# Two layers of attention on one core: layer 1's maxima and sums sent through DRAM, its weights a step later

## The chip, the cores and the metric

The kernel runs on one core of one Trainium2 chip. The metric is the time of one execution on the device in microseconds (us). The profile is of one further execution; the engines are named as in it: PE (matrix products), PEld (its weight loads), DVE (vector), ACT (scalar), POOL (GpSimd) and SP (here only a queue for DMAs).

## The reference, cut to what matters

Two attention layers over an image of 2 x 256 x 64 x 64 in float32, that is 2 batches of N = 4096 positions with 256 channels. Layer 0 (layer norm, four heads of 16 channels, a gate, a sigmoid) is not touched. Layer 1 is this:

```
qkv = einsum('oc,bchw->bohw', w_qkv, x) + b_qkv        # 4 heads, each 3 x 64 channels
q, k, v = split(qkv.reshape(b, 4, 192, 4096), 3, axis=2)
attn = softmax(einsum('bhdn,bhdm->bhnm', q, k) / sqrt(64), axis=-1)
out = einsum('bhnm,bhdm->bhnd', attn, v).reshape(b, c, h, w)
return einsum('oc,bchw->bohw', w_out, out) + b_out + x
```

## The kernel before, in words

Layer 1 works through 32 units `(b, g, j)`: a batch, a pair of heads, and a block of NB = 512 queries. A unit has NM = 32 chunks of 128 keys. A chunk's scores for both heads are one tile of 128 keys x (2 heads x 512 queries). Two chunks are done in one step `t`, so a unit takes 16 steps, and the body of layer 1 has 512.

The softmax subtracts a maximum, and it does so by halves: the 16 chunks of a half (`GS`) share one maximum for each query and head. A half's exponentials can't begin before its last scores are in, so scores run ahead: the shift and the exponential of a chunk come `LAG` = 10 steps after its scores, and the product with the values one step later. In between the scores lie in a ring of 2 LAG + 4 = 24 buffers in SBUF.

For each chunk:

- PE multiplies keys by queries into a "pair" buffer in PSUM (`score`, L861). There are two of these, of two banks each.
- DVE takes the running maximum over the chunks, element by element (`keep`, L878), and ACT copies the scores into the ring (L879). The copy waits for the maximum of the same chunk, and PE's scores two chunks on wait for the copy.
- LAG steps later DVE adds the negated maximum (`shift`, L944), ACT takes the exponential in place (`weigh`, L956), POOL adds it to an accumulator, from which the sum over the keys is made (L966 for the first two chunks of a half in one instruction, L968 for the others), and PE multiplies it with the values (`gather`, L978).

At the end of each half the maxima go through this chain:

1. `turn_max` (L886): PE transposes the 512 columns of one head into the single "misc" bank of PSUM, and `fold` (L898) lets DVE take the negated maximum over the 128 keys. This is done for one head at the step's "early" place and for the other at its "late" place.
2. `split` (L909 to L912): POOL takes each maximum apart into three bf16 pieces.
3. `turn` (L925, L930), a step later: PE turns the pieces into rows, ACT copies these to SBUF.
4. `spread_shift` (L939), a further step later: PE multiplies the rows by ones, which adds the pieces up and puts the result on all 128 partitions, in the single "shift" buffer of PSUM.

At the end of a unit, in steps 12 to 14 of the next one, come the sums. `total` (L1008): PE sums the accumulators over the partitions. `keep_total` (L1016): ACT copies that. `turn_total` (L1023): PE turns it. `factors` (L1035 to L1039): DVE joins the sums of the two halves and takes the reciprocal, POOL makes the other half's factor. `turn_sums` (L1023) and `rows` (L1049, L1056, L1060): PE turns the products with the values, DVE scales them, POOL adds the bias and the two halves together, and SP sends the result to DRAM (L1076). The last unit's rows go straight into the SBUF tile from which the last output is made (L1067).

Beside this, other steps hang in the loop: the queries of the next unit (`next_queries`, L672, at steps 14 and 15), and, in the first 24 units, keys and values for the unit eight further on (L672 and L705, at steps 4 to 7), which go to DRAM and are fetched back. During four units of the second batch the first batch's output is made as well (`project_out`, L1083, and `output`, L1091).

The order is written out by hand. `at(t, place, step)` hangs a step on a step number and a place (start, early, early end, late, late end), the main loop (L1219) runs through them, and `seq` keeps each engine's instructions in the program's order. Each engine, and SP, therefore takes its instructions one after the other: what waits holds up all that is behind it on the same engine. Tiles come from pools: a new tile in a pool waits until an older one's readers are done.

Of the kernel before, what the change touches and what calls it, by code (L numbers as in the profile page):

```python
# [9 lines left out]
BF16 = mybir.dt.bfloat16  # L10
# [17 lines left out]
def conv_attention_kernel(  # L28
# [149 lines left out]
    def layer1_constants():  # L178
# [25 lines left out]
        ident16 = const.tile([P, P], BF16, tag="ident16", name="ident16")  # L204
        nc.gpsimd.tensor_copy(ident16, ident)
        ones16 = const.tile([P, P], BF16, tag="ones16", name="ones16")
        nc.gpsimd.memset(ones16, 1.0)
        ones = const.tile([P, D1], F32, tag="ones", name="ones")
        nc.gpsimd.memset(ones, 1.0)


        negmax1 = []
        for i in range(2):
            t = const.tile([P, PB, P], BF16, tag=f"negmax1_{i}", name=f"negmax1_{i}")
            nc.gpsimd.memset(t, 0.0)
            negmax1.append(t)
        return w1, wo1, b1, b1v, bo1, ident16, ones16, ones, negmax1
# [27 lines left out]
    with own0:  # L245
# [412 lines left out]
        w1, wo1, b1, b1v, bo1, ident16, ones16, ones, negmax1 = layer1_constants()  # L658
# [109 lines left out]

    units = [(b, g, j) for b in range(B) for g in range(PR) for j in range(NJ)]
    GS = NM // 2  # L770
    NG = NM // GS
    LAG = GS // 2 + 2
# [5 lines left out]
    with (  # L778
# [9 lines left out]
        rmax, negs, mrows, shifts, raws, accs = {}, {}, {}, {}, {}, {}  # L788
        avs1, srows, losts, joined, halves = {}, {}, {}, {}, {}
        rts = [None, None]  # L790
# [10 lines left out]
        )  # L801
        last_att = []
# [78 lines left out]
        def turn_max(u, n, k):  # L881

            b, g, j = u
            ps = misc(f"rt_{b}_{g}_{j}_{n}_{k}")
            for i in range(PB):
                seq(nc.tensor.transpose(  # L886
                    ps[:, bass.ts(i, P)], rmax[u, n][:, k, bass.ts(i, P)], ident
                ))
            rts[k] = ps

        def fold(u, n, k):

            b, g, j = u
            if k == 0:
                negs[u, n] = small.tile(
                    [P, 2, PB], F32, tag="negs", bufs=2 * NG, name=f"negs_{b}_{g}_{j}_{n}"
                )
            seq(nc.vector.tensor_reduce(  # L898
                negs[u, n][:, k, :], rts[k].rearrange("p (i m) -> p i m", m=P), AX.X, ALU.max,
                negate=True,  # L900
            ))

        def split(u, n):

            b, g, j = u
            nm = negs[u, n]
            to = negmax1[n % 2].rearrange("p i (k e) -> p k i e", e=D1)
            rest = small.tile([P, 2, PB], F32, tag="rest1", name=f"rest1_{b}_{g}_{j}_{n}")
            seq(nc.gpsimd.tensor_copy(to[:, :, :, 0], nm))  # L909
            seq(nc.gpsimd.tensor_tensor(rest, nm, to[:, :, :, 0], ALU.subtract))  # L910
            seq(nc.gpsimd.tensor_copy(to[:, :, :, 1], rest))
            seq(nc.gpsimd.tensor_tensor(to[:, :, :, 2], rest, to[:, :, :, 1], ALU.subtract))  # L912
            if n == 1:

                lost = small.tile([P, 2, PB], F32, tag="lost", name=f"lost_{b}_{g}_{j}")
                seq(nc.gpsimd.tensor_tensor(lost, nm, negs.pop((u, 0)), ALU.subtract))
                negs.pop((u, 1))
                losts[u] = lost

        def turn(u, n):  # L920

            b, g, j = u
            ps = misc(f"nm1p_{b}_{g}_{j}_{n}")
            for i in range(PB):
                seq(nc.tensor.matmul(  # L925
                    ps[:, bass.ts(i, P)], negmax1[n % 2][:, i, :], ident16,
                    start=True, stop=True,
                ))
            mrows[u, n] = l1.tile([P, NB], BF16, tag="mrow", name=f"mrow_{b}_{g}_{j}_{n}")
            seq(nc.scalar.copy(mrows[u, n], ps))  # L930

        def spread_shift(u, n):

            b, g, j = u
            ps = psb.tile([P, 2, NB], F32, tag="shift", name=f"shift_{b}_{g}_{j}_{n}")
            row = mrows.pop((u, n))
            for k in range(2):
                r = slice(k * D1, (k + 1) * D1)
                seq(nc.tensor.matmul(ps[:, k, :], ones16[r, :], row[r, :], start=True, stop=True))  # L939
            shifts[u, n] = ps  # L940
# [72 lines left out]
        def keep_total(u):  # L1013
            b, g, j = u
            row = l1.tile([P, NB], F32, tag="srow", bufs=1, name=f"srow_{b}_{g}_{j}")
            seq(nc.scalar.copy(row, srows[u]))  # L1016
            srows[u] = row
            seq(nc.scalar.activation(losts[u], losts[u], AF.Exp, scale=D1**-0.5))

        def turned(a, name):  # L1020
            ps = misc(name)
            for i in range(PB):
                seq(nc.tensor.transpose(ps[:, bass.ts(i, P)], a[:, bass.ts(i, P)], ident))  # L1023
            return ps.rearrange("p (i k d) -> p i k d", k=2, d=D1)

        def turn_total(u):
            srows[u] = turned(srows[u], "sumt_{}_{}_{}".format(*u))

        def factors(u):

            b, g, j = u
            ps = srows.pop(u)
            lost = losts.pop(u).rearrange("p k i -> p i k")
            s = small.tile([P, PB, 2], F32, tag="sum1", name=f"sum1_{b}_{g}_{j}")
            seq(nc.vector.tensor_tensor(s, ps[:, :, 0, ::32], lost, ALU.mult))  # L1035
            seq(nc.vector.tensor_tensor(s, s, ps[:, :, 1, ::32], ALU.add))
            f = small.tile([P, NG, PB, 2], F32, tag="f1", name=f"f1_{b}_{g}_{j}")
            seq(nc.vector.reciprocal(f[:, 1], s))
# [6 lines left out]
        def rows(u, n):  # L1045
            b, g, j = u
            ps = avs1.pop((u, n))
            r = l1.tile([P, PB, 2, D1], F32, tag="rows", name=f"rows_{b}_{g}_{j}_{n}")
            seq(nc.vector.tensor_tensor(  # L1049
                r, ps, joined[u][:, n].unsqueeze(3).to_broadcast([P, PB, 2, D1]), ALU.mult  # L1050
            ))
            last = u == units[-1]
            if n == 1:
                halves[u] = r
                bias = b1v[:, 2 * g : 2 * g + 2, :].unsqueeze(1).to_broadcast([P, PB, 2, D1])
# [7 lines left out]
            if last:  # L1063
                for k in range(2):
                    c = ((2 * g + k) * N + j * NB) // D1 % P
                    for i in range(PB):
                        (nc.sync if k else nc.scalar).dma_start(  # L1067
                            out=last_att[0][c + 2 * i : c + 2 * i + 2, :].rearrange(
                                "q (s d) -> q s d", d=D1
                            ),  # L1070
                            in_=r[:, i, k, :],
                        )
                return
            to = att[b].rearrange("(h q) (s d) -> h (q s) d", h=H, d=D1)
            for k in range(2):
                nc.sync.dma_start(  # L1076
                    out=to[2 * g + k, bass.ts(j, NB), :].rearrange("(i q) d -> q i d", q=P),
                    in_=r[:, :, k, :],
                )

# [18 lines left out]
        def fetch_output(b, j):  # L1099
            fetch(("xo", b, j), x1[b][j], "xo", 2, l1)  # L1100
# [8 lines left out]
        for n, u in enumerate(units):  # L1109
            b, g, j = u  # L1110
            t0 = n * US
            if n > 0:
                at(t0 - 5, "start", lambda u=u, b=b, j=j: fetch(("q", u), x1[b][j]))
                at(t0 - 2, "late", lambda u=u: next_queries(u, 0))
                at(t0 - 1, "early", lambda u=u: next_queries(u, 1))
                at(t0 - 1, "early end", lambda u=u: keep_queries(u))
            if n < len(units) - NJ:
                to = (*units[n + NJ][:2], j)
                at(t0 + 1, "start", lambda to=to: fetch(("kv", *to), x1[to[0]][to[2]]))
# [185 lines left out]
```

## Time and profile before

| | us |
|---|---|
| median of 3 runs (lowest, highest) | 4742.67 (4740.17, 4742.81) |
| the profiled execution | 4741.58 |
| its span | 4739.8 |
| PE busy in the span | 4526.9 (96%) |
| DVE busy | 3917.0 (83%) |
| ACT busy | 3394.1 (72%) |
| POOL busy | 2540.6 (54%) |

The shares are means over both layers. Layer 1's loop begins near 2050 us and its last instructions end the run; POOL and DVE do most of their work there. The mean time of one instruction in layer 1: an accumulation on POOL 2.37 us, a shift 1.21, a maximum 1.22, a fold 0.69, a copy of scores on ACT 1.01, an exponential 1.06. In an answer of the trace each line of a timeline has its start, its length, engine, line, operation, what it writes and reads, and, in brackets, how long the engine stood idle before it and who released it. In a line of waits stand who waited for whom, the total, how often, and the longest.

### The profile page before, as it was taken

What the parts mean: (1) busy time and instruction counts of PE and PEld (TensorE: products, weight loads), DVE (VectorE), ACT (ScalarE), POOL (GpSimd) and SP (SyncE); (2) the same over time, 40 slices, a digit from 0 to 9 for tenths busy, and PEclk for the clock granted to TensorE, in tenths of its full rate; (3) what the DMA queues carried; (4) which work ended last, traced back from release to release, by engine and by line L of the source; (5) the groups of instructions that cost most, each with busy time, mean ns of one, the idle gap of its engine ahead of it and who ended that gap; (6) DMA issues with size and microseconds to landing.
All of it is one profiled execution on the core that took longest, in us unless ns stands there. A gap on an engine that the chain in (4) does not pass through costs nothing.

```text
span 4739.8 us, 70643 instructions
## 1 busy us (share of the span) xinstructions
PE 4526.9 (96%) x27506; PEld 1496.2 (32%) x27506; DVE 3917.0 (83%) x4584; ACT 3394.1 (72%) x4508; POOL 2540.6 (54%) x1491
## 2 busy tenths in 40 slices
PE   8999999999999999989999999999999999999998
PEld 3433333333333333333232232323233332222222
DVE  6777777777777777359999999999999899999996
ACT  3366666666666666668888888888887778888884
POOL 6300000000000000039999999999998889999994
PEclk9999999999999999999999999999999999999999
DMA  3100000000000000110000100001111111000002
GB/s 103 34 4 19 19 21 15 15 15 15 15 15 15 15 13 13 57 63 25 23 25 17 54 30 23 25 23 36 52 36 45 63 52 47 18 14 7 14 16 74
DMA packets 113381, 140.10 MB, mean 30 GB/s; under 512 B 51864, under 2 KB 52696, under 8 KB 112932
## 3 DMA queue, kind: packets, MB, share of 16 engines
q1 hardware_dynamic: 111260, 135.11, 9.2%
q8 instruction: 216, 3.54, 0.3%
q14 instruction: 121, 0.99, 0.1%
q10 hardware_dynamic: 1784, 0.46, 0.0%
HBM read 93.58 MB, written 41.70 MB: 29 GB/s over the span
## 4 chain that ended last, share of the span: by engine, by line
PE 58%; DVE 15%; POOL 15%; issue 6%; ACT 5%; DMA 1%; SPq 0%; ACTq 0%; DVEq 0%; POOLq 0%
PE s L448 24%; POOL acc L968 13%; PE av L463 12%; DVE rmax L878 10%; PE s L861 6%; PE av L978 5%; DVE raw L944 4%; ACT raw L879 4%; PE a L410 2%; PE p L270 1%; PE k1p L672 1%; POOL acc L966 1%; PE rt L886 1%; PE q1p L672 1%; PE o L549 1%
## 5 line engine op out<-in xcount | busy, mean ns | idle before, releaser
L968 POOL TENSOR_TENSOR acc<-acc,raw 128x1024 f32<-128x1024 f32 x884 | 2098.1, 2373 | 89.4 <-ACT raw L956 30.2
L414 DVE TENSOR_REDUCE mx<-a 128x1 f32<-128x512 f32 x2048 | 1315.3, 686 | 450.5 <-PE a L410 449.4
L451 ACT ACTIVATE p<-s 128x512 f32<-128x512 f32 x2048 | 1109.8, 597 | 701.3 <-PE a L410 367.3
L944 DVE TENSOR_TENSOR raw<-raw,shift 128x1024 f32<-128x1024 f32 x1024 | 1238.0, 1213 | 19.2 <-PE shift L939 12.7
L861 PE MATMUL s<-q,k 64*128 64x512 f32 x4096 | 1117.2, 636 | 142.9 <-ACT raw L879 134.6
L878 DVE TENSOR_TENSOR rmax<-s,rmax 128x1024 f32<-128x1024 f32 x960 | 1170.1, 1219 | 72.7 <-PE s L861 70.8
L879 ACT COPY raw<-s 128x1024 f32<-128x1024 f32 x1024 | 1037.7, 1013 | 259.4 <-DVE rmax L878 173.5
L448 PE MATMUL s<-q,kT 32*128 32x512 f32 x4096 | 1219.1, 640 | 0.0
L956 ACT ACTIVATE raw<-raw 128x1024 f32<-128x1024 f32 x1024 | 1086.9, 1062 | 178.4 <-DVE raw L944 147.3
L410 PE MATMUL a<-kT,q 32*128 32x512 f32 x4096 | 1129.7, 643 | 1.2 <-DVE mx L414 1.0
L978 PE MATMUL av<-raw,v 128*64 128x512 f32 x4096 | 999.3, 606 | 2.0
L463 PE MATMUL av<-p,v 128*32 128x256 f32 (+1 forms) x7904 | 650.2, 399 | 0.6 <-ACT avs L477 0.6
L861 PEld LDWEIGHTS s<-q,k 64*128 64x128 f32 x4096 | 317.1, 185 | 827.9 <-ACT raw L879 628.0
L513 POOL TENSOR_TENSOR f<-f,dyn 128x16 f32<-128x16 f32 x15 | 3.3, 223 | 1028.2 <-DVE f L512 1028.2
L448 PEld LDWEIGHTS s<-q,kT 32*128 32x128 f32 x4096 | 397.9, 183 | 426.3 <-issue 392.1
L978 PEld LDWEIGHTS av<-raw,v 128*64 128x64 f32 x4096 | 243.3, 136 | 587.6 <-issue 428.8
L463 PEld LDWEIGHTS av<-p,v 128*32 128x32 f32 x7904 | 157.6, 108 | 751.5 <-issue 737.3
L564 POOL TENSOR_SCALAR res<-res 128x1024 f32<-128x1024 f32 x16 | 16.8, 1049 | 660.5 <-ACT res L563 660.5
L410 PEld LDWEIGHTS a<-kT,q 32*128 32x128 f32 x4096 | 305.0, 184 | 31.4 <-DVE mx L414 18.2
L966 POOL TENSOR_TENSOR acc<-raw,raw 128x1024 f32<-128x1024 f32 x64 | 152.4, 2381 | 112.7 <-ACT raw L956 103.8
L898 DVE TENSOR_REDUCE negs<-rt 128x4 f32<-128x512 f32 x128 | 88.3, 690 | 50.1 <-PE rt L886 47.6
L318 DVE RECIPROCAL std<-std 128x128 f32<-128x128 f32 x64 | 56.1, 920 | 37.7 <-ACT std L313 37.7
(332 smaller groups left out, 1840.4 us busy)
## 6 DMA issues: line engine op xcount, KB each, us to landing
x<-in_x_dram SPq DMA_DIRECT2D x16, 512.0 KB
res<-in_x_dram SPq DMA_DIRECT2D x16, 512.0 KB
x<-res SPq DMA_DIRECT2D x16, 512.0 KB
att<-rows SPq DMA_DIRECT2D x62, 128.0 KB
kd<-k1s SPq DMA_DIRECT2D x24, 256.0 KB
vd<-v1s SPq DMA_DIRECT2D x24, 256.0 KB
k<-kd SPq DMA_DIRECT2D x24, 256.0 KB
v<-vd SPq DMA_DIRECT2D x24, 256.0 KB
```

The lines of the kernel that those rows point to most:

```text
L410: seq(nc.tensor.matmul(ps, qs0[u][r, bass.ts(i, P)], kTs[b][r, bass.ts(m, NB)], start=True, stop=True,))
L414: seq(nc.vector.tensor_reduce(mxs[u][:, i * H + h, m : m + 1], ps, AX.X, ALU.max))
L448: seq(nc.tensor.matmul(ps, kTs[b][r, bass.ts(m, P)], qs0[u][r, :], start=True, stop=True))
L451: seq(nc.scalar.activation(pt[:, k, :], ps, AF.Exp, scale=D0**-0.5))
L463: seq(nc.tensor.matmul(avs[u][32 * h : 32 * h + 32, cols], vs0[b][:, m, 32 * h : 32 * h + 32], pts[t, h // 2][:, h % 2, cols], start=(m == ...
L861: seq(nc.tensor.matmul(ps[:, k, :], ks[b, g, m // PB][r, bass.ts(m % PB, P)], qs1[u][r, :], start=True, stop=True,))
L878: seq(nc.vector.tensor_tensor(rmax[u, n], ps, before, ALU.max))
L879: seq(nc.scalar.copy(raw, ps))
L944: seq(nc.vector.tensor_tensor(raws[t], raws[t], shifts[u, t % NM // GS], ALU.add))
L956: seq(nc.scalar.activation(p, p, AF.Exp, scale=D1**-0.5))
L968: seq(nc.gpsimd.tensor_tensor(accs[u, n], accs[u, n], p, ALU.add))
L978: seq(nc.tensor.matmul(avs1[u, n][k * D1 : (k + 1) * D1, :], v[:, m % PB, k, :], raws[t][:, k, :], start=(m % GS == 0), stop=(m % GS == GS ...
```

## The change

The bf16 pieces and what belongs to them (`split`, `turn`, `spread_shift` and their constants) are taken out. `turn_max` transposes both heads at once into a "pair" buffer, taking every fourth query in a transpose, and one `fold` does both. SP sends the negated maxima to DRAM and reads them back onto all partitions (`row`); ACT copies that row into the "shift" buffer three steps after the fold (`place_shift`). LAG becomes 11, the ring gets 26 buffers. The sums go to DRAM and back as well, in place of `turn_total`, and two of the operations in `factors` move from DVE to POOL. Queries, keys, values and the outputs of the first batch are hung on other steps; there is one "xo" buffer in place of two. The last unit's rows go through DRAM.

```diff
-    LAG = GS // 2 + 2
+    LAG = GS // 2 + 3
...
+        def by_query(a, i):
+            return a.rearrange("p (q i) -> p i q", i=PB)[:, i, :]
...
+        def turn_max(u, n):
             b, g, j = u
-            ps = misc(f"rt_{b}_{g}_{j}_{n}_{k}")
-            for i in range(PB):
-                seq(nc.tensor.transpose(
-                    ps[:, bass.ts(i, P)], rmax[u, n][:, k, bass.ts(i, P)], ident
-                ))
-            rts[k] = ps
+            ps = psp.tile([P, 2, NB], F32, tag="pair", name=f"rt_{b}_{g}_{j}_{n}")
+            for k in range(2):
+                for i in range(PB):
+                    seq(nc.tensor.transpose(
+                        ps[:, k, bass.ts(i, P)], by_query(rmax[u, n][:, k, :], i), ident
+                    ))
+            rts[u] = ps
...
+        def fold(u, n):
+            nm = small.tile([P, 2, PB], F32, tag="negs", bufs=2 * NG, name=f"negs_{b}_{g}_{j}_{n}")
             seq(nc.vector.tensor_reduce(
-                negs[u, n][:, k, :], rts[k].rearrange("p (i m) -> p i m", m=P), AX.X, ALU.max,
-                negate=True,
+                nm, rts.pop(u).rearrange("p k (i m) -> p k i m", m=P), AX.X, ALU.max, negate=True,
             ))
+            to = neg1[u, n]
+            nc.sync.dma_start(out=to.rearrange("k (p i) -> p k i", i=PB), in_=nm)
+            row = l1.tile([P, 2, NB], F32, tag="row", bufs=1, name=f"row_{b}_{g}_{j}_{n}")
+            nc.sync.dma_start(
+                out=row.rearrange("p k n -> p (k n)"),
+                in_=to.rearrange("(o k) n -> o (k n)", o=1).partition_broadcast(P),
+            )
+            rows_in[u, n] = row
...
+        def place_shift(u, n):
             b, g, j = u
             ps = psb.tile([P, 2, NB], F32, tag="shift", name=f"shift_{b}_{g}_{j}_{n}")
-            row = mrows.pop((u, n))
-            for k in range(2):
-                r = slice(k * D1, (k + 1) * D1)
-                seq(nc.tensor.matmul(ps[:, k, :], ones16[r, :], row[r, :], start=True, stop=True))
+            seq(nc.scalar.copy(ps, rows_in.pop((u, n))))
             shifts[u, n] = ps
...
         def keep_total(u):
-            row = l1.tile([P, NB], F32, tag="srow", bufs=1, name=f"srow_{b}_{g}_{j}")
+            row = l1.tile([P, NB], F32, tag="kv", name=f"srow_{b}_{g}_{j}")
             seq(nc.scalar.copy(row, srows[u]))
-            srows[u] = row
+            for m in range(2 * NG):
+                nc.sync.dma_start(out=sum1[u][m : m + 1, :], in_=row[32 * m : 32 * m + 1, :])
+            s = small.tile([P, NG, 2, PB], F32, tag="sums1", name=f"sums1_{b}_{g}_{j}")
+            nc.sync.dma_start(
+                out=s.rearrange("p n k i -> p (n k) i"),
+                in_=sum1[u].rearrange("m (p i) -> p m i", i=PB),
+            )
+            srows[u] = s
...
         def factors(u):
-            seq(nc.vector.tensor_tensor(s, ps[:, :, 0, ::32], lost, ALU.mult))
-            seq(nc.vector.tensor_tensor(s, s, ps[:, :, 1, ::32], ALU.add))
-            f = small.tile([P, NG, PB, 2], F32, tag="f1", name=f"f1_{b}_{g}_{j}")
-            seq(nc.vector.reciprocal(f[:, 1], s))
+            seq(nc.gpsimd.tensor_tensor(s[:, 0], s[:, 0], lost, ALU.mult))
+            seq(nc.gpsimd.tensor_tensor(s[:, 1], s[:, 1], s[:, 0], ALU.add))
+            f = small.tile([P, NG, 2, PB], F32, tag="f1", name=f"f1_{b}_{g}_{j}")
+            seq(nc.vector.reciprocal(f[:, 1], s[:, 1]))
             seq(nc.gpsimd.tensor_tensor(f[:, 0], f[:, 1], lost, ALU.mult))
...
             for k in range(2):
-                nc.sync.dma_start(
-                    out=to[2 * g + k, bass.ts(j, NB), :].rearrange("(i q) d -> q i d", q=P),
-                    in_=r[:, :, k, :],
+                queue = (nc.sync, nc.scalar)[k if last else 0]
+                queue.dma_start(
+                    out=to[2 * g + k, bass.ts(j, NB), :].rearrange("(p i) d -> p i d", i=PB),
+                    in_=r[:, k, :, :],
                 )
+                if last:
+                    c = ((2 * g + k) * N + j * NB) // D1
+                    queue.dma_start(
+                        out=last_att[0][c % P : c % P + NB // D1, :],
+                        in_=att[b][c : c + NB // D1, :],
+                    )
...
-                at(t0 - 2, "late", lambda u=u: next_queries(u, 0))
-                at(t0 - 1, "early", lambda u=u: next_queries(u, 1))
-                at(t0 - 1, "early end", lambda u=u: keep_queries(u))
+                for c in range(CC):
+                    at(t0 - 6 + c, "early", lambda u=u, c=c: next_queries(u, c))
+                at(t0 - 5, "early end", lambda u=u: keep_queries(u))
...
-                    at(t0 + 4 + c, "early", lambda to=to, c=c: next_keys(*to, c))
-                at(t0 + 5, "early end", lambda to=to: store_keys(*to))
-                at(t0 + 6, "early", lambda to=to: next_values(*to, 0))
-                at(t0 + 7, "early", lambda to=to: next_values(*to, 2))
-                at(t0 + 7, "early end", lambda to=to: store_values(*to))
+                    at(t0 + 2 + c, "early", lambda to=to, c=c: next_keys(*to, c))
+                at(t0 + 3, "early end", lambda to=to: store_keys(*to))
+                at(t0 + 5, "early", lambda to=to: next_values(*to, 0))
+                at(t0 + 6, "early", lambda to=to: next_values(*to, 2))
+                at(t0 + 6, "early end", lambda to=to: store_values(*to))
...
-                at(t1, "early", lambda u=u, k=k: turn_max(u, k, 0))
-                at(t1, "early end", lambda u=u, k=k: fold(u, k, 0))
-                at(t1, "late", lambda u=u, k=k: turn_max(u, k, 1))
-                at(t1, "late end", lambda u=u, k=k: (fold(u, k, 1), split(u, k)))
-                at(t1 + 1, "late", lambda u=u, k=k: turn(u, k))
-                at(t1 + 2, "early", lambda u=u, k=k: spread_shift(u, k))
+                at(t1, "early", lambda u=u, k=k: turn_max(u, k))
+                at(t1, "early end", lambda u=u, k=k: fold(u, k))
+                at(t1 + 3, "start", lambda u=u, k=k: place_shift(u, k))
             t1 = t0 + US + GS // 2
             at(t1 + 4, "early", lambda u=u: total(u))
             at(t1 + 4, "early end", lambda u=u: keep_total(u))
-            at(t1 + 5, "early", lambda u=u: turn_total(u))
-            at(t1 + 5, "early end", lambda u=u: factors(u))
-            at(t1 + 5, "late", lambda u=u: turn_sums(u, 1))
-            at(t1 + 5, "late end", lambda u=u: rows(u, 1))
-            at(t1 + 6, "early", lambda u=u: turn_sums(u, 0))
-            at(t1 + 6, "early end", lambda u=u: rows(u, 0))
+            at(t1 + 6, "start", lambda u=u: factors(u))
+            for place, k in (("early", 1), ("late", 0)):
+                at(t1 + 6, place, lambda u=u, k=k: turn_sums(u, k))
+                at(t1 + 6, f"{place} end", lambda u=u, k=k: rows(u, k))
```

## The prediction

> **What bounds the kernel now.** First the busy share by stretch of the run, one line each from the body of layer 1 and from its last quarter (columns: stretch, length, then PE, weight loads, DVE, ACT, POOL, each with its instruction count, clock, DMA share, GB/s).
>
> ```profile
> 3000.00:3300.00 300.00, 283.74 (x1212) 90.57 (x1210) 280.81 (x267) 251.91 (x269) 280.05 (x156) 1.00 0.09 26
> 4200.00:4500.00 300.00, 275.75 (x1168) 82.17 (x1168) 288.06 (x274) 257.94 (x270) 286.42 (x158) 1.00 0.04 11
> ```
>
> PE, DVE and POOL are all at 93 to 96%, so shares don't say who is the bound. The waits between 2100 and 4600 us do (total, times, longest):
>
> ```profile
> DVE rmax L878 <- PE s L861: 66.3, 134, 0.9
> POOL acc L966 <- ACT raw L956: 92.0, 61, 2.5
> DVE negs L898 <- PE rt L886: 45.3, 61, 1.0
> ```
>
> POOL, once per half unit, has emptied its queue and waits 1.5 us for the first exponentials of the next half (L966). It is not ahead of anybody, but it isn't behind either: it follows DVE. So I read DVE's order of instructions in one unit; a unit of 16 steps runs from the fold at 3059.20 to the same one at 3140.64, 81.44 us.
>
> ```profile
> 3058.07 1.21 DVE L944 TENSOR_TENSOR raw<-raw,shift 128x1024 f32<-128x1024 f32 x1
> 3059.20 0.68 DVE L898 TENSOR_REDUCE negs<-rt 128x4 f32<-128x512 f32 x1
> 3059.80 1.22 DVE L878 TENSOR_TENSOR rmax<-s,rmax 128x1024 f32<-128x1024 f32 x1
> 3061.16 0.69 DVE L898 TENSOR_REDUCE negs<-rt 128x4 f32<-128x512 f32 x1
> ...
> 3067.42 1.22 DVE L878 TENSOR_TENSOR rmax<-s,rmax 128x1024 f32<-128x1024 f32 x1
> 3068.98 1.22 DVE L944 TENSOR_TENSOR raw<-raw,shift 128x1024 f32<-128x1024 f32 x1 [0.34 <-POOL acc L968]
> ...
> 3080.30 1.21 DVE L944 TENSOR_TENSOR raw<-raw,shift 128x1024 f32<-128x1024 f32 x1
> 3082.11 1.23 DVE L878 TENSOR_TENSOR rmax<-s,rmax 128x1024 f32<-128x1024 f32 x1 [0.60 <-PE s L861]
> ```
>
> Start to start, a shift or a maximum takes 1.13 us, a fold 0.60. 32 shifts and 31 maxima (71.4), four folds (2.4), two `rows` (1.2) and the three factor operations (0.5) make 75.6. The other 5.9 us are gaps in front of something late: 0.2 and 1.7 at the two pairs of folds (the second pair is the one at 3099.93 and 3102.38), 0.4 twice at the first shift of a half, 0.7 after the sums on PE, 2.2 behind the keys and values on PE, 0.3 elsewhere. DVE's order, with its gaps, is the clock of this stage; in the last quarter, without keys and values, DVE's sum (79.3) and POOL's (78.9 with 0.07 us between instructions) meet, and the unit takes 79.2.
>
> [...] the trace's exponential, from SBUF, takes 1.06. [...] in layer 0 a factor row is issued at 705.99 and its read-back at 708.24. [...] No PE read in the trace of before strides 16 bytes[...].
>
> **Part by part**, per unit, as changes of DVE's gaps.
>
> *Folds.* Two reduces of 1024 replace four of 512: 2.4 to 2 x 1.13 (priced as a tensor_tensor of that size), -0.14. The two small factor operations go to POOL: -0.4. Busy: -0.54.
>
> *The turned maxima move to a "pair" buffer.* Both pair buffers hold the scores of this step, so PE's transposes must wait for ACT's copy of the first. First half's end: the maximum starts at 3056.93 and ends 3058.16, ACT copies until 3059.2, eight transposes take 1.24 (two times the 0.65 of four, less overlap), the fold can start at 3060.6 where DVE is ready at 3059.2: wait 1.4, before 0.22, so +1.18. Second half's end: maximum 3095.47 to 3096.70, copy to 3097.7, exponential to 3098.9, copy of the new unit's first scores to 3099.9, transposes to 3101.2; DVE is ready at 3098.95: 2.35 against 1.69, +0.66. Queued behind the fold on DVE are the next maximum and shift, and behind the transposes on PE the gather; PE catches up behind the fold. If the 16-byte stride doubles the transposes, each wait grows by 1.2.
>
> *The shift is placed by ACT, a step later.* Its buffer (one) is free when DVE's last shift of the old half ends; ACT first does that chunk's exponential (1.06), then the copy into PSUM [...], while DVE has one maximum to do (1.06 more). Wait 1.1 instead of 0.4: +0.7, twice a unit. The row must be there[...]; DVE's order gives it 2.5 steps, some 12 us. [...]
>
> *The factors.* This is the largest. Before, DVE formed the sum itself. Now POOL multiplies and adds (two operations), and DVE's reciprocal waits for POOL, whose queue is in order: in front stand the accumulations of all chunks up to the one DVE has just shifted. What POOL has in hand there:
>
> ```profile
> 3073.99 2.38 POOL L966 TENSOR_TENSOR acc<-raw,raw 128x1024 f32<-128x1024 f32 x1 [2.54 <-ACT raw L956]
> 3076.45 12.17 POOL L968 TENSOR_TENSOR acc<-acc,raw 128x1024 f32<-128x1024 f32 x5
> 3088.58 0.20 POOL L1039 TENSOR_TENSOR f<-f,lost 128x8 f32<-128x8 f32 x1
> ```
>
> POOL is empty when the half's first accumulation (chunks 0 and 1, one instruction) comes; up to chunk 5 it needs 5 x 2.43, until 3086.15. The shift of chunk 5 starts at 3080.30 and DVE would take its next instruction at 3081.43: POOL is 4.7 us behind. Add two small operations at 0.28, subtract the gap of 0.68 behind the sums, which in the new order lies ahead of that shift: 4.6 us, each unit. Behind the reciprocal on DVE stand maximum, shift and `rows`; for the maximum waits ACT's copy, for that PE's scores. Bounds: 2 us if DVE arrives later through gaps I haven't seen, 5.5 with the sums' DMA late. That DMA (four issues, 1.39 us in layer 0[...]) has 9 us.
>
> *Moved PE work.* Queries go to steps 10 and 11 as an "early" step: a half before the gather costs 0.74 for keys, the second half lies in the placing's stall: 0.74 against 0.11, +0.63. The second half of the keys now lies in the other placing's stall: -0.27. Turned sums hide behind the reciprocal: -0.3. The removed PE work (turn, spread, turned totals, about 2.2 us) and POOL's four split operations with their gaps (2.3) are on engines that wait for DVE: nothing. [...] SP gets nine more issues a unit, under 4 us of 80, and each neg write is queued behind the att write, which waits for POOL's rows; those end at 3096 where the fold is at 3099.93, so nothing.
>
> *Ends.* LAG of 11 costs a step of drain, about 2.9 (gather 1.87 and sums 0.98); [...] the last rows now go out and back in four DMAs[...] where eight took from 4704.95 to 4718.5[...]. Sum 0.
>
> **Sum.** Reciprocal 31 x 4.6 = 143, less 8 in the four units of the output stage, where an output's wait ahead of it eats 1.9 each time; folds 31 x (1.18 + 0.66) = 57; placing 62 x 0.7 = 43; queries 20; busy -17; keys -6; turned -9. Together +223 on the profiled execution's 4741.6 (span 4739.8), which lies 1.1 under the median: 4965.
>
> **Rivals.** *Only the stalls at the folds and the placing count*: POOL would be relieved enough, or DVE late enough, that the reciprocal waits little. Without its 135: 4830. For it: POOL loses 1.8 us of work a unit. Against: it is already empty at each half's start, so it can't be further ahead. *The stride doubles the transposes*: 62 x 1.2 on top, 5040. [...] against it that weight loads (0.14) and transposes overlap. *Faster*: POOL is the bound, and DVE's new waits fall into time that it has spare anyway. Then POOL's relief counts, four split operations out, two in, 1.77 us x 32 = 57: 4685. It speaks for it that POOL's sum equals the unit's time in the last quarter, where DVE's 3.6 us of gaps cost nothing by themselves. It decides only if DVE's added waits stay under POOL's slack, 81.4 - 78.9 = 2.5 us a unit, and I count 7. *The change does nothing*: hardly, since the instructions do change; 2%.
>
> **How the numbers follow.** Likeliest (66%) 4965, its own range 4880 to 5030; without the reciprocal 14% at 4830; strided 13% at 5040; faster 5%; same 2%. About 0.2% is what a measurement of this kernel can tell from no change. The range 4850 to 5060 leaves out the faster and the same case, most of the second rival and a fifth of the third: 19%. Faster 0.05, same 0.02, slower 0.93.
>
> **What would show it.** In the trace of after: DVE's reciprocal idle 4 to 5 us, released by POOL's sums; the fold waiting 1.4 and 2.4 us for its transposes, PE's transposes for ACT's copy; the first shift of a half waiting 1 us for ACT; POOL idle longer than before; the unit at 88 us. Wrong if the unit stays under 82, if ACT waits for a row's DMA, or if eight transposes take over 2 us.

## The result and the profile after

The changed kernel takes 4988.99 us (median of 4 runs, 4982.25 to 4990.93) beside 4741.93 for the kernel before on the same chip: ratio 1.0519, 95% interval 1.0505 to 1.0534. The profiled execution has a span of 4988.7 us, 248.9 more than before.

The busy shares in the same two stretches as before (stretch, length, then PE, weight loads, DVE, ACT, POOL, each with its count, clock, DMA share, GB/s):

```profile
3000.00:3300.00 300.00, 263.50 (x1050) 86.78 (x1052) 257.73 (x232) 235.56 (x247) 250.89 (x122) 0.95 0.11 33
4200.00:4500.00 300.00, 255.05 (x994) 79.63 (x992) 258.07 (x232) 234.83 (x241) 251.90 (x121) 0.94 0.09 25
```

Every engine does less in 300 us, and PE's granted clock, 1.00 in both stretches before, is 0.95 and 0.94. No engine has taken over as the bound, so something waits. DVE's waits between 2100 and 4893 us (total, times, longest):

```profile
DVE f L1022 <- POOL sums L1020: 134.5, 31, 4.4
DVE negs L898 <- PE rt L888: 129.1, 62, 2.9
DVE rmax L875 <- PE s L858: 97.5, 163, 1.0
DVE raw L925 <- ACT shift L920: 17.4, 57, 1.0
```

The first line is new, once per unit. The folds' line was 46.3 before up to the same point of the work, the maxima's 67.2; the last line stands in place of 16.6 us of waits before the first shift of a half. No wait of ACT for a row's DMA appears. One unit's timeline shows where the two large ones lie:

```profile
3080.15 1.21 DVE L925 TENSOR_TENSOR raw<-raw,shift 128x1024 f32<-128x1024 f32 x1
3085.76 0.20 DVE L1022 RECIPROCAL f<-sums 128x8 f32<-128x8 f32 x1 [4.40 <-POOL sums L1020]
...
3095.44 2.34 DVE L925 TENSOR_TENSOR raw<-raw,shift 128x1024 f32<-128x1024 f32 x2
3100.71 1.22 DVE L898 TENSOR_REDUCE negs<-rt 128x8 f32<-128x1024 f32 x1 [2.93 <-PE rt L888]
```

Two instructions of 0.2 and 1.2 us hold up DVE for 7.3 us. The fold in the middle of the unit waits another 1.31. A unit of 16 steps takes 88.7 us, before 81.4; in the last quarter 88.7, before 79.2.

Why does the fold at the unit's end wait 2.93, when the fold in the middle waits 1.31? PE's own timeline, and then six stretches of its clock (the number after POOL's count). The trace records the granted clock as 1.00 or 0.50 only, each, up to the run's last stretch, for 3.41 us or a multiple of it, so the stretches are laid on this grid:

```profile
3088.85 1.13 PE L1011 MATMUL turned<-ident,avs 128*128 128x128 f32 x4 [3.79 <-DVE rows L1033]
3098.69 1.98 PE L888 MATMUL rt<-ident,rmax 128*128 128x128 f32 x8 [0.89 <-ACT raw L876]
```

```profile
3081.64:3085.06 3.42, 3.42 (x16) 1.09 (x14) 0.00 (x0) 0.81 (x1) 3.34 (x2) 1.00 0.00 0
3085.06:3088.47 3.41, 0.00 (x1) 0.00 (x0) 2.71 (x4) 1.25 (x2) 0.79 (x4) 1.00 0.00 0
3088.47:3091.88 3.41, 3.03 (x10) 1.62 (x12) 3.26 (x4) 1.83 (x2) 2.52 (x2) 0.50 0.00 0
3091.88:3095.30 3.42, 3.42 (x18) 0.93 (x14) 3.28 (x4) 2.95 (x3) 3.34 (x3) 1.00 0.03 9
3095.30:3098.71 3.41, 1.63 (x9) 0.32 (x5) 2.48 (x3) 3.22 (x5) 3.33 (x2) 1.00 0.22 72
3098.71:3102.12 3.41, 3.41 (x12) 2.10 (x14) 1.41 (x2) 0.89 (x1) 3.25 (x3) 0.50 0.00 0
```

Beside the reciprocal's stall PE stands still for 3.79 us, and in the next stretch its clock is 0.50. Here the fall follows a long gap. But one stretch later the clock is back at 1.00. The half clock under the eight transposes, which take 1.98 us, is a second fall. It follows a stretch without any such gap, in which PE worked only 1.63 of 3.41 us and twice waited 0.89 for ACT's copy. In the middle of the unit, at full clock, the transposes take 1.24. So the fold's long wait isn't what is left of the reciprocal's stall; the experiments bear this out.

### The profile page after: what moved, and what is told of

It is laid out like the page before. It is cut to its first block, busy times and chain, and to the rows that moved or that the text cites. A ratio compares the mean times of both kernels' runs of the same rounds, so it can differ in the third digit from the quotient of the medians.

```text
span 4988.7 us, 69799 instructions
## 1 busy us (share of the span) xinstructions
PE 4573.0 (92%) x26998; PEld 1533.3 (31%) x26998; DVE 3908.3 (78%) x4456; ACT 3427.6 (69%) x4508; POOL 2499.0 (50%) x1294
## 5 line engine op out<-in xcount | busy, mean ns | idle before, releaser
L858 PE MATMUL s<-q,k 64*128 64x512 f32 x4096 | 1149.2, 654 | 192.2 <-ACT raw L876 188.5
L959 PE MATMUL av<-raw,v 128*64 128x512 f32 x4096 | 1021.8, 620 | 1.7 <-ACT avs L976 1.7
L858 PEld LDWEIGHTS s<-q,k 64*128 64x128 f32 x4096 | 333.0, 192 | 979.4 <-ACT raw L876 715.7
L959 PEld LDWEIGHTS av<-raw,v 128*64 128x64 f32 x4096 | 255.6, 140 | 627.5 <-issue 529.6
L898 DVE TENSOR_REDUCE negs<-rt 128x8 f32<-128x1024 f32 x64 | 78.4, 1224 | 131.5 <-PE rt L888 131.5
L1011 PE MATMUL turned<-ident,avs 128*128 128x128 f32 x256 | 59.6, 370 | 116.6 <-DVE rows L1033 116.6
```

The source lines that it names most:

```text
L858: seq(nc.tensor.matmul(ps[:, k, :], ks[b, g, m // PB][r, bass.ts(m % PB, P)], qs1[u][r, :], start=True, stop=True,))
L959: seq(nc.tensor.matmul(avs1[u, n][k * D1 : (k + 1) * D1, :], v[:, m % PB, k, :], raws[t][:, k, :], start=(m % GS == 0), stop=(m % GS == GS ...
```

## The experiments

My theory after the result: DVE's in-order list sets the pace of layer 1; the reciprocal's wait for POOL's list, the fold's wait for the shared pair buffers and a lower PE clock behind the first make nearly all of the loss. The first two held; of the third only a part did. Rivals: the sums' DMA is what the reciprocal waits for; the strided transposes are slow; the row through DRAM is late.

**POOL's two operations back on DVE.**

```diff
-            seq(nc.gpsimd.tensor_tensor(s[:, 0], s[:, 0], lost, ALU.mult))
-            seq(nc.gpsimd.tensor_tensor(s[:, 1], s[:, 1], s[:, 0], ALU.add))
+            seq(nc.vector.tensor_tensor(s[:, 0], s[:, 0], lost, ALU.mult))
+            seq(nc.vector.tensor_tensor(s[:, 1], s[:, 1], s[:, 0], ALU.add))
```

> The changed kernel with the multiply and the add of the sums back on DVE (two operations of 0.16 us each); sums still go through DRAM. Theory (DVE's reciprocal waits 4.48 us a unit for POOL's queue, and PE, idle meanwhile, comes back at a lower clock): 31 x (4.48 - 0.40) = 126 us less, and about 1 us a unit less at the turned sums and the next fold: 4833 us (4815 to 4865). No idle of DVE in front of the reciprocal. Rival (POOL's queue is late anyway and the wait comes back at the next thing that needs POOL, the rows or the ring): 4940 to 4990.

Measured: 4876.45 (ratio to before 1.0283, 1.0268 to 1.0299). The reciprocal's wait is gone, 112 us gained, 43 less than expected and outside the stated range. The multiply, which reads what the sums' DMA brought, starts without a wait, so that DMA doesn't hold the reciprocal. Two things are behind the missing 43. The multiply on DVE has a price of its own (below). And the folds' waits stay: 123.5 us in all, from 129.1, though no reciprocal waits any more. So the stall of the step before isn't what makes them long.

**The maxima turned head by head again**, in the misc bank with two folds, the stride and everything else as changed (`turn_max` and `fold` get back their argument for the head, hung on "early" and "late").

> The changed kernel with the maxima turned one head at a time in the misc bank, two folds of 512 at the early and the late end, as before; everything else as changed, the transposes still take every fourth query. Theory (the folds wait because the transposes need a pair buffer, which is free only after ACT's copy of this step's first scores): the two folds' waits go from 1.31 + 2.93 us to about 0.2 + 1.7, two folds more cost 0.14: 31 x 2.2 = 68 us less, 4921 us (4900 to 4945). Rival (the folds wait because the transposes themselves are slower, by the stride or the clock): 4975 to 4990.

Measured: 4907.04 (1.0351, 1.0334 to 1.0369), 82 us gained where I expected 68. The folds' waits in all fall from 129.1 to 61.0 us. The stride is still there, so it wasn't the cost. The edit undoes two things at once, the shared pair buffer and the turning of both heads in one go. The trace of the change speaks for the buffer, since between 2100 and 4600 us its transposes wait for ACT's copy of the scores (total, times, longest):

```profile
PE rt L888 <- ACT raw L876: 56.1, 56, 1.1
```

What each of the two is worth by itself wasn't separated.

**Both.**

> Both edits of the two runs ahead of this one together. Theory: the two causes add up, 4833 - 52 = 4781 us (4750 to 4815); what is left over the kernel before is the placing, the queries in front of it and the end. Rival (a third wait takes their place, POOL or ACT becoming the bound): above 4830.

Measured: 4805.29 (1.0136, 1.0121 to 1.0151), clock 0.994. Together the two gain 184 us, three quarters of the loss; singly they gained 112 and 82. The 24 us short of the expectation lie within what the multiply costs. Here it is, with POOL's list beside it:

```profile
3109.03 1.59 DVE L1022 TENSOR_TENSOR sums<-sums,lost 128x8 f32<-128x8 f32 x1
3110.66 0.17 DVE L1023 TENSOR_TENSOR sums<-sums 128x8 f32<-128x8 f32 x1
```

```profile
3103.34 9.73 POOL L952 TENSOR_TENSOR acc<-acc,raw 128x1024 f32<-128x1024 f32 x4
```

The kernel before did a multiply of the same size, with one operand in PSUM, in 0.16 us. POOL's four accumulations, 2.43 each from 3103.34, change over at 3110.63, and the multiply ends at 3110.62. In 27 of the 32 units the multiply takes 1.59 us, in the four that make the first batch's output 0.42. In the last unit, where POOL has nothing in hand, it takes 0.17:

```profile
4772.29 0.17 DVE L1022 TENSOR_TENSOR sums<-sums,lost 128x8 f32<-128x8 f32 x1 [3.92 <-DMA sums<-sum_(1, 1, 7)_19383]
```

Where the multiply took 1.59 us, both its inputs lay in SBUF, POOL was adding in SBUF beside it, and the two ended together. So the theory was that such a multiply waits for POOL's running accumulation. It was tested with **the factor in PSUM**: ACT writes exp(lost) into the sums' bank as well, in 27 of the 32 units, and DVE's product goes there too.

```diff
+                sp = srows[u][:, : 2 * PB].rearrange("p (k i) -> p k i", k=2)
+                seq(nc.scalar.activation(sp, losts[u], AF.Exp, scale=D1**-0.5))
...
-            seq(nc.vector.tensor_tensor(s[:, 0], s[:, 0], lost, ALU.mult))
-            seq(nc.vector.tensor_tensor(s[:, 1], s[:, 1], s[:, 0], ALU.add))
+            seq(nc.vector.tensor_tensor(sp, s[:, 0], sp, ALU.mult))
+            seq(nc.vector.tensor_tensor(s[:, 1], s[:, 1], sp, ALU.add))
```

> As e3_both (4805), but for 27 of the 32 units ACT writes the factor exp(lost) into PSUM as well, and DVE's multiply and add take one operand from PSUM and one from SBUF. Theory (a DVE operation with two SBUF operands waits for POOL's running accumulation, the 1.59 us in front of every multiply but the last, where POOL was idle and it took 0.17): the multiply takes 0.16 to 0.2, the add too, the unit falls by 1.4: 4805 less 27 x 1.43, 4766, 4756 to 4782. Rival (the multiply is slow because it is the first reader of what a DMA wrote, or for its form): it still takes 1.5 us, 4800 to 4810.

Measured: 4770.11 (1.0062, 1.0045 to 1.0079), 35 us gained. In the groups of instructions (count, then busy, mean ns of one, and the idle time before):

```profile
L1031 DVE TENSOR_TENSOR sum<-sums,sum 128x8 f32<-128x8 f32 x27 | 4.4, 164 | 0.1
L1032 DVE TENSOR_TENSOR sums<-sums,sum 128x8 f32<-128x8 f32 x27 | 4.4, 162 | 0.9
```

One input and the product are now in PSUM, and ACT makes one more exponential; the shape and the DMA-written input are the same, and 1.59 became 0.16. The rivals, a first read of what a DMA wrote or the form of the instruction, are out.

**Is it POOL's operations or their place?** On top of the head-by-head turning, the two operations stay on POOL but are hung a step earlier.

```diff
-            seq(nc.gpsimd.tensor_tensor(s[:, 0], s[:, 0], lost, ALU.mult))
-            seq(nc.gpsimd.tensor_tensor(s[:, 1], s[:, 1], s[:, 0], ALU.add))
...
+            at(t1 + 5, "start", lambda u=u: join_sums(u))
             at(t1 + 6, "start", lambda u=u: factors(u))
```

> The change, with the maxima turned head by head as in e2_turn_by_head (4907), and POOL's two sum operations hung one step (two chunks) ahead of the reciprocal; no arithmetic moves to DVE. Theory (DVE waits only because POOL's list, two accumulations of 2.43 us behind DVE, lies ahead of the two operations[...]): in e2 the read-back is issued at 3050.39[...], POOL's accumulation ahead of the new place ends at 3053.3, DVE asks at 3054.2, so the wait of 4.4 us goes and nothing takes its place: 4907 less 31 x 4.4, 4771, less some us for the PE clock that no longer falls behind the stall: 4760, 4740 to 4785. Rival (the sums' DMA is the true bound of the reciprocal): POOL waits for it in front of the accumulations, DVE still waits 1 to 2 us: 4800 to 4850.

Measured: 4770.21 (1.0062, 1.0047 to 1.0077), 137 us less than the same kernel without the edit. POOL, then DVE:

```profile
3090.45 0.20 POOL L1020 TENSOR_TENSOR sums<-sums,lost 128x8 f32<-128x8 f32 x1
3090.74 0.20 POOL L1021 TENSOR_TENSOR sums<-sums 128x8 f32<-128x8 f32 x1
```

```profile
3090.26 1.21 DVE L928 TENSOR_TENSOR raw<-raw,shift 128x1024 f32<-128x1024 f32 x1
3091.39 0.19 DVE L1029 RECIPROCAL f<-sums 128x8 f32<-128x8 f32 x1
```

The sums are there 0.45 us before DVE asks. Two accumulations fewer ahead of two small instructions are worth the whole wait: it was queueing, neither the sums' DMA nor POOL's speed. A little queueing is left behind the reciprocal: the second `rows` of a unit needs the factor that POOL makes, and DVE waits for it 26 times, 11.6 us up to 4620, where the change had no such wait.

**The clock by itself.** On the change as it is, useless matmuls (their result is overwritten) fill PE's idle time ahead of the turned sums; first six, then three.

```diff
+            for _ in range(busy):
+                seq(nc.tensor.matmul(ps, ident, a, start=True, stop=True))
```

> The changed kernel with six matmuls of 128x512 without use (about 3.2 us of PE) into the bank of the turned sums just before these are turned, so that PE has work while DVE waits for POOL; the output doesn't change. Theory (PE's idle time of 3.8 us a unit brings the granted clock down to 0.58 to 0.65 of full speed some us later, which lengthens the turned sums and the transposes in front of the fold): the fold's wait at the unit's end goes from 2.93 to about 2.35 us, the reciprocal's stays at 4.4; 1 us a unit, 4958 us (4945 to 4970). Rival (the clock costs nothing, since DVE waits for something else): 4985 to 5000.

Measured: 4984.71 (1.0514, 1.0498 to 1.0530), no gain to speak of. The fold's wait did fall from 2.93 to 2.19 in the unit shown above, and over the whole run from 129.1 to 118.1. But the six took 5.42 us, 0.9 each where I had reckoned 0.53, and ended after the reciprocal: DVE's waits in front of the rows grew from 1.1 to 32.9 us, some 1.1 a unit.

> The change with three matmuls of no use (their result is overwritten; 128x512, measured at 0.9 us each in e4_pe_filled) ahead of the turned sums, in the 3.8 us in which PE stands still beside the waiting reciprocal. Theory (that idle time costs granted clock, which makes the fold behind it wait 2.9 where 2.2 would do, and three end before the reciprocal): 31 x 0.6 less, 4970, 4955 to 4980. Rival (the clock fall is not from this idle time): 4985 to 4990.

Measured: 4946.29 (1.0435, 1.0419 to 1.0450), 43 us less than the change, more than the 19 expected. PE and the clock behind it:

```profile
3077.11 0.75 PE L1013 MATMUL turned<-ident,avs 128*128 128x128 f32 x4 [1.19 <-DVE rows L1035]
3086.47 1.24 PE L888 MATMUL rt<-ident,rmax 128*128 128x128 f32 x8 [0.89 <-ACT raw L876]
```

```profile
3075.00:3078.00 3.00, 1.81 (x12) 0.81 (x10) 3.00 (x4) 2.07 (x2) 0.38 (x1) 1.00 0.00 0
```

With three matmuls of no use the kernel is faster: the idle time is 1.19 instead of 3.79 us, the clock stays at 1.00, and in this unit the transposes are back at 1.24. Not in all: 8 of 31 folds at a unit's end still wait over 2.5 us. Over the run the folds' waits fall by 15 us, the maxima's by 6, the outputs' by some 5; most of what is left of the 43 stands in no line of the list of waits.

The long idle time isn't the only cause of a fall, as the first experiment shows. No reciprocal waits there, PE is never idle for more than 1.12 us in the 25 us before, and yet its eight transposes take 1.67 us ahead of the fold at 3063.69:

```profile
3059.13:3062.55 3.42, 1.69 (x8) 0.86 (x9) 1.95 (x2) 3.36 (x4) 3.34 (x2) 1.00 0.23 75
3062.55:3065.96 3.41, 3.41 (x12) 1.47 (x12) 2.27 (x2) 0.35 (x1) 3.25 (x3) 0.50 0.03 1
```

When the clock falls can be counted. The traces of all fourteen kernels, from 2100 us to 110 us before the end, have 10,544 stretches of 3.41 us at full clock, and behind 141 of them it falls to half. In all 141 PE was busy, as the trace counts it, for at most 53% of the stretch. Of those in which it was busy for less than 44% all 74 are followed by a fall, of those between 44% and 53.5% 67 of 84, of the 10,386 busier ones none. So what these kernels show is a share of work in a fixed stretch: the gap of 3.79 us is one way to fall below it, two waits of 0.89 us in the same stretch are another. The change has 62 such falls, the kernel before none. This also says why the fillers must be read with care. In the change most falls come 23 and 3 stretches apart, which is 88.75 us, almost exactly its unit of 88.73, so they strike the same place of each unit. With three fillers the unit is 87.2 us, no multiple of a stretch, so each unit lies differently on the grid, and 10 falls are left, about one in every third unit. How much of the 43 us is the filled gap and how much the new position on the grid wasn't separated.

**The placing.** In the last quarter, where no projection makes PE late in the same step, the first shift of a half does wait 0.90 for ACT's copy. If it waits because ACT does the last exponential first, the copy belongs ahead of it:

```diff
-                at(t1 + 3, "start", lambda u=u, k=k: place_shift(u, k))
+                at(t1 + 2, "last", lambda u=u, k=k: place_shift(u, k))
```

("last" is a new place, behind the step's second shift.)

> As e6_sums_pool_early (4770), but ACT places the row right behind DVE's last shift of the old half, ahead of that chunk's exponential instead of behind it. Theory (the first shift of a half waits because ACT does 1.06 us of exponential before the 1.0 us copy, while DVE has 1.13 us of other work): the waits of 0.30 and 0.23 in a unit with keys and values and of 0.99 in a unit of the last quarter go, 22 x 0.53 + 8 x 1.29 = 22 less: 4748, 4742 to 4758. Rival (ACT's list is what is full there, so the exponential comes late instead and PE's products and POOL's sums behind it): 4765 or more.

Without it, ACT and then DVE at such a place:

```profile
4443.56 1.06 ACT L940 ACTIVATE raw<-raw 128x1024 f32<-128x1024 f32 x1
4444.53 1.01 ACT L923 COPY shift<-row 128x1024 f32<-128x1024 f32 x1
```

```profile
4445.57 1.22 DVE L928 TENSOR_TENSOR raw<-raw,shift 128x1024 f32<-128x1024 f32 x1 [0.90 <-ACT shift L923]
```

Measured: 4752.72 (1.0022, 1.0013 to 1.0030), 17 us gained. A half of 36.66 us of the last quarter becomes 35.71, and the shift no longer waits. With queries or keys in the step the gain is small: at step 11 the shift's wait of 0.22 goes, but the maximum behind it now waits 0.23 for PE's scores.

**The end of the run.** The last unit's sums are transposed by PE and joined by DVE as before, a step earlier.

```diff
+            if u == units[-1]:
+                srows[u] = row
...
+                return
```

> As e6_sums_pool_early, and for the last unit alone the sums aren't sent through DRAM but transposed by PE and joined by DVE, a step ahead. Theory (the 13 us that the end of the run grew by are the sums' DMAs queued behind the loads of the last stage): 12 us less than e6_sums_pool_early, about 4748, 4728 to 4773; in the trace the last reciprocal comes 10 to 12 us sooner after the last shift. Rival (the loads of the last x chunks bound the end anyway): less than 4 us gained.

Measured: 4767.67 (1.0057, 1.0042 to 1.0072), 2.5 us gained: the expectation failed. The reciprocal does come 12 us earlier, but then:

```profile
4721.72 0.20 DVE L1044 RECIPROCAL f<-sums 128x8 f32<-128x8 f32 x1
4728.31 1.41 DVE L1204 SCALAR_TENSOR_TENSOR x_last<-o,bo,x_last 128x512 f32<-128x512 f32 x2 [6.39 <-DMA x_last<-x]
4729.63 0.68 DVE L1055 TENSOR_TENSOR rows<-turned,f 128x512 f32<-128x512 f32 x1
```

The rows, which don't need the load of x, stand behind an addition that does. So the next kernel hangs these additions behind the rows:

```diff
-            (END + GS // 2 + 5, "early end"): (5,), (END + GS // 2 + 6, "early end"): (6, 7),
+            (END + GS // 2 + 6, "late end"): (5, 6, 7),
```

> As e7_and_tail (4768), but the last unit's rows stand on DVE ahead of the three additions to x chunks whose loads come last. In e7 the last reciprocal came 12 us sooner and the first of the rows then waited behind an addition that waited 6.4 us for its load. Theory (the end of the run is bound by the last rows' way out and back, 11.8 us, and only the order on DVE kept the 12 us): 4757, 4752 to 4762. Rival (the loads of x bound the end by themselves): 4764 or more.

Measured: 4760.25 (1.0040, 1.0026 to 1.0054), another 7 us. Together 10 of the 13 us that the end had grown by.

**All together**, the placing and the end on top of the early sums. The maxima are still turned head by head and the last unit's sums don't go through DRAM, so it is what is left of the change.

> e10_place_first and e11_rows_before_fill together. If both theories hold their gains add: 4770 - 22 - 13 = 4735, 4727 to 4748, which would be the first of these kernels not slower than the kernel before (4741). If either falls, 4750 or more.

Measured: 4742.47 (1.0001, 0.9993 to 1.0010): no difference from the kernel before. So the change's own idea, one turn through DRAM in place of PE's and POOL's work, costs next to nothing once its stalls are gone, and gains nothing either as far as it was taken: the waits of `rows` for POOL's factor, 12.3 us up to 4620, are still in it.

**One further step**, on the gaps that the kernel before has too, 0.74 and 0.32 us on DVE behind each pair of projection chunks: each chunk cut into pieces of half the columns and spread over more steps (`project_piece` in `next_queries` and `next_keys`, values one block at a time).

> As e12_all (4742), but the queries' projection is cut into four pieces of half the columns, one a half step where it can be (steps 9, 10 and 11), and so are keys and values of all units but those of the output stage (steps 1 to 3 and 4 to 7). Theory (a chunk of projection in one step makes PE's step 4.84 us against DVE's 4.53, and each such step shows a gap of 0.74 and then 0.32 on DVE; a piece of half the length leaves PE's step at 4.3): most of the gaps go, 31 x 1.07 for queries and 22 x 2.2 for keys and values, at most 81 less; some gap stays where two pieces share a step: 4690, 4670 to 4720, which would beat the kernel before (4741). Rival (DVE isn't late for PE's amount of work but for the switch of PE to other weights and back, once per piece): more switches, no gain, 4740 or more.

Measured: 4723.77 (0.9964, 0.9950 to 0.9978), the only kernel here faster than the kernel before; the gain of 19 us is under half of the 52 expected and misses the stated range. It is no credit to the change, since the pieces weren't tried on the kernel before. A piece of values on PE:

```profile
3036.30 0.71 PE L693 MATMUL v1p<-w,xb_('kv', 1, 0, 4)_24804 128*128 128x128 f32 x4
3036.95 1.94 PE L970 MATMUL av<-raw,v 128*64 128x512 f32 x8
```

A piece takes 0.65 us until PE's next instruction where half a chunk would be 0.53, and 0.23 to 0.54 us of wait stay in most steps that have a piece. That is in between the theory and its rival; what of it is the switch and what the length wasn't separated.

## Why the prediction was right, and where not

The forecast was 4965, the result 4989, inside the range; the mechanism, DVE's list and what it waits for, held. One mechanism has no term in it, PE's clock, which counted for nothing and did cost time. By the steps of its sum, from the wait totals of both traces:

| step | predicted | measured |
|---|---|---|
| reciprocal behind POOL's list | 135 | 134.5 |
| folds behind the pair buffers | 57 | 129.1 - 46.3 = 83 |
| placing by ACT | 43 | 17.4 - 16.6 = 1 |
| queries and keys on other steps | 14 | 97.5 - 67.2 = 30 |
| turned sums | -9 | 1.1 - 2.0 = -1 |
| outputs | no term | 14.5 - 20.4 = -6 |
| DVE's own work | -17 | -16 |
| end of the run | 0 | 96.5 - 83.1 = 13 |
| sum | 223 | 239, of 248.9 |

DVE's own work is 0.4 for two operations, 31 times, and 0.06 for a fold, 62 times. That turned sums and outputs together come near the -9 is luck. The 10 us that are left aren't in these waits. With three fillers some 15 us went that no line of the list holds either, so part of the 10 may be short delays from PE's clock; that isn't shown.

- *The reciprocal*: cause and size as predicted, POOL's sums ahead of it in POOL's list, which was shown by moving the two operations up that list. The exact sum is in part luck: the wait is 4.38 in 27 units, not 4.6, and 4.06 in the four units with an output, so that the discount of 8 us for these measured 1.3.
- *The folds*: 1.4 in the middle of the unit, measured 1.31, and 2.35 at its end, measured 2.19 where PE's clock is full. But it isn't in 24 of the 31 ends, where the wait is 2.75 to 2.93, nor in the middle of the units of the last quarter, 1.76 to 1.91. What is above 2.19 and 1.31 makes 21 of the 129.1 us. Without it, 108 - 46.3 = 62 stand against the 57 predicted. The stride, the rival at 5040, costs little: four transposes take 0.75 us, before 0.65.
- *PE's clock*: the two falls of most units, behind the reciprocal's stall and behind the shared pair buffers, weren't foreseen. Besides the 21 us at the folds, some 6 of the maxima's 30 went when most falls were gone. With 52 of the 62 falls gone, the kernel with three fillers was 43 us faster; how much of that is the clock alone wasn't separated.
- *The placing* was the mis-sized term. Its 0.7 us, twice a unit, counted as if nothing else was late there; ACT's copy itself takes 1.01 us, the mean of 64, about as long as an exponential (1.06). But queries and keys in the same step make PE late by 0.66, ACT's copy lies beside that, and only 0.15 to 0.22 is left. Where PE isn't late, 0.90 is there. I took both the queries' 0.63 and the placing's 0.7 as losses of one step; only the larger counts. In the other direction, I put the second halves of queries and keys into the placing's stall for nothing, and that stall hardly exists: their 14 became 30.
- *The end* was the step that I closed at 0, from 2.9 for the longer LAG, more for the sums' DMAs and less for the rows' DMAs; what the DMAs would take was an estimate of mine, not read from a trace. It came out at 13. From the last fold to the last shift it takes 4.8 longer; from the last rows to the first of the last additions 11.9, before 17.5, so that gain was there (-5.6). But the last reciprocal comes 26.6 after the last shift, before 13.1: the four DMAs of the sums take 4.85 us to issue, behind two loads of 896 KB and three of 512 KB in SP's queue, and their read-back is issued 13.7 us after the first, against 2.03 to 2.74 in the body of the run. My estimate counted nothing ahead of them in the queue. On DVE an addition that waits 7.69 for its load of x stands ahead of the same reciprocal, which then waits only 3.99 for POOL's sums. This fits the mere 2.5 us that earlier sums alone gained.

One reading of the trace was wrong as well. The 2.25 us from a factor row's issue to its read-back don't show what a small DMA takes: four other issues stand between the two in SP's queue, and the last of them ends at 708.19. The trace of after comes nearer to it: the maxima's read-back is issued 1.55 to 3.26 us after the issue of the write that it needs (median 2.19 of 64), the sums' 1.16 to 1.87 us after the last of their four writes (median 1.26, the last unit left out).

Two of the errors had opposite signs (placing -42; folds, queries and end together +55), which brought the sum nearer than its terms deserve.

## What to carry to other kernels

Two small operations moved to a less busy engine cost 135 us, since that engine's queue was two long instructions behind the one that asks: when work is moved, count what is queued ahead of it there, and ask for it that much earlier. Losses in one step don't add up; take the largest, and look what is late next. Look at what short waits do to the next stretch: behind two of 0.89 us eight transposes took 1.98 us instead of 1.24, at half the clock. In these traces, wherever PE worked less than 44% of a 3.41 us stretch of layer 1, the next one ran at half the clock. Read the granted clock on the grid of its own changes; the 0.58 and 0.65 in my expectations are means over stretches that lay across it.

## What was not expected of the hardware

- A DVE multiply of 128x8 with both inputs in SBUF took 1.59 us beside a running POOL accumulation, 0.17 with POOL idle, and 0.16 with one input and the product in PSUM; 31 units made 44 us of it.
- PE's granted clock was 1.00 or 0.50, in stretches of 3.41 us on a fixed grid. In fourteen traces all 141 falls came behind a stretch in which PE was busy for at most 53%, whether it held a gap of 3.79 us or none over 1.12, and none of the 10,386 stretches above 53.5% was followed by one. At half clock eight 128x128 transposes took 1.98 us instead of 1.24.
- Three useless 128x512 matmuls a unit made the kernel 43 us faster.
- A 128x512 matmul of fp32 took 0.9 us in a row of six.
